# Who issues the row loads of the first expert layer's early tiles, behind which fence, and when the ends of the lists are written

## The chip, the core and the metric

The kernel runs on one core of a Trainium2 chip. The metric is device time in microseconds (us), from one execution of the whole program; lower is better. Before the change three runs took 1994.12, 1999.18 and 2002.74 us; their median, 1999.18 us, is the time before.

The engines are called as the profile calls them: PE (matmul; PEld loads its stationary operand), DVE (vector), ACT (scalar: activation functions, copies), POOL (general purpose; it also issues the indirect transfers here), SP (issues transfers and computes nothing). ACT and SP issue plain transfers. ACTq and SPq mark what the engine's sequencer does: waits, register work, transfers that it issues.

## What is computed

Four layers on 8 x 512 tokens of 256 numbers, each with a residual and a layer norm behind it: three gated recurrent layers, a mixture of 8 experts in which each expert chooses its tokens, attention with a relative bias, and a mixture of 16 experts in which each token has four. Only the second layer and what lies just before it matter here:

```python
probs = softmax(xt @ Wg)                       # 4096 tokens, 8 experts
top_idx = top_k(probs.T, T // E)               # each expert picks 512 tokens
tok2exp = argmax(where(selected, probs.T, -inf), axis=0)   # then each token has one expert
for e in range(E):
    gate = where(tok2exp == e, weights, 0.0)
    out = out + gate[:, None] * (gelu(xt @ W1[e]) @ W2[e])
x = layernorm(x + out)
```

## The kernel before

The program is written in Python and fully unrolled; a scheduler orders the instructions of each engine, except where a block takes the order as written.

**Lists.** Once each token has its expert, the tokens are sorted into lists, one for each expert, in device memory (`m0rows`, class `Lists`). A row is 276 float32 numbers: 256 of the token, its gate and its number. POOL writes the rows with 32 indirect transfers of 128 rows (`put`, L722); each token's place has been computed by DVE (L1113 to L1116, `slot`). A list is rarely a multiple of 128 long, so behind each list's last row 128 empty rows are written (`end_list`, L755 to L759): eight plain transfers by SP, whose address is loaded to a register from the table `m0end` (L750). The lists are then worked on in tiles of 128 rows of one expert. DVE builds a table that says for each tile where its rows begin and which expert's weights it needs (`table`, L781 to L814).

**Early tiles.** Once half of the puts (16) have landed, some tiles are known to be full whatever the other half brings: NE0 = 8 of the 39 tiles are taken from these, the early tiles. Their loads wait for a fence, an instruction that waits for these 16 puts (`fence`, L736 to L746). Before the change it is a copy of one column on ACT (L741), and the loads of the eight early tiles (`load`, L886 to L899) are issued by ACT, those of all later tiles by SP. The later tiles wait for a second fence on POOL (L743, `close`), behind all puts and all ends of lists.

**A tile** (`run`): two transposes of its rows on PE (L903, `m0xp`), a copy to SBUF by DVE (L905, `m0xq`), the first product (L916, `m0h`: four banks of PSUM, eight matmuls, which the trace counts as sixteen), four gelus on ACT that free these banks (L924, `m0hT`), the second product (L938, `m0o`), gate and residual on DVE (L1145, `z`), and an indirect transfer on POOL that puts the rows back in token order (L1148, `res`, called the scatter below). There are only four banks for `m0h`, so the first product of a tile needs the gelus of the tile before it.

**What sets the order.** Four weight buffers (`m0ws`, 1034 KB each) are filled by SP (L882, L884), the first four before all else; a buffer is refilled when the tile four before it is done with it, and from the second round on only if the expert changes. There are five row buffers, so tile 5's load waits for the scatter of tile 0 (which reads its row's token number from that buffer), tile 6's for that of tile 1, and so on. Each engine's instructions run in order, so a load that waits holds back everything behind it on the engine that issues it. In the order of the built kernel, ACT's part is: fence, loads of tiles 0 to 4, table of the gelu function, gelus of tiles 0 to 2, load of tile 5, gelus of tile 3, loads of tiles 6 and 7, gelus of tile 4. SP's part is: weights of tiles 0 to 3, the eight ends of lists (called from `besides` at tile 0), weights of tiles 4 to 7, then a load and its weights in turn. PE's part is: transposes of tiles 0 and 1, first products of tiles 0 and 1, transposes of tile 2, second product of tile 0, first product of tile 2, and so on.

A plain transfer tells of its landing by one of eight semaphores taken in turn, and is not issued before that semaphore's earlier transfer has landed. In the kernel before, the second and third end of a list so wait for ACT's loads of tiles 0 and 1.

Of the kernel before, what the change touches and what calls it, by code (L numbers as in the profile page):

```python
# [46 lines left out]
NE0 = (NC // 2 * P - E0 * (P - 1)) // P  # L47
# [632 lines left out]
class Lists:  # L680
# [53 lines left out]
            tc.declare_no_dep(ins, load, reason="of rows written before")  # L734
        self.written.append(ins)

    def fence(self, on_act=False):

        full = self.rp.tile([P, 1], F32, name=f"{self.name}full{len(self.written)}")
        if on_act:  # L740
            ins = self.nc.scalar.copy(full, self.pno).ins  # L741
        else:
            ins = self.nc.gpsimd.memset(full, 0.0).ins  # L743
        for w in self.written:
            self.tc.add_manual_dep(ins, w.name, SYNC, reason="the lists are full")
        return ins  # L746

# [110 lines left out]
    def run(self, ctx, ident, w_pack, bias, done, taken=None, besides=None):  # L858

        tc, nc, E, NT, nm = self.tc, self.nc, self.E, self.NT, self.name
        table, value, weights_of = self.of, self.value, self.weights_of
        wp = ctx.enter_context(tc.tile_pool(name=f"{nm}w", bufs=1))
        hp = self.hp
        psX = ctx.enter_context(tc.tile_pool(name=f"{nm}psX", bufs=2, space=PSUM))
        psH = ctx.enter_context(tc.tile_pool(name=f"{nm}psH", bufs=4, space=PSUM))
        psO = ctx.enter_context(
            tc.tile_pool(name=f"{nm}psO", bufs=1 if bias else 2, space=PSUM)
        )  # L870
        ws = [None] * len(self.held) + [
            wp.tile([P, WPK], F32, name=f"{nm}ws{i}") for i in range(len(self.held), NW)
        ]
        ws[: len(self.held)] = self.held
        xgs, hTs = {}, {}

        def weights(t):
            if t < len(self.held):
                return
            w = weights_of(t, w_pack)  # L880
            if t - table(t)[0] < NW:
                nc.sync.dma_start(ws[t % NW], w)  # L882
            else:
                nc.sync.dma_start(ws[t % NW], w, cond=value(t, 2, 1))  # L884

        def load(t):  # L886
            xgs[t] = hp.tile([P, RW], F32, tag="xg", bufs=NW + 1, name=f"{nm}xg_{t}")

            q = nc.sync if bias or t >= self.early else nc.scalar
            at = value(t, 0, E * LT, q.engine)  # L890
            ins = q.dma_start(xgs[t], self.rows[bass.ds(at, P), :]).ins
            if t < self.early:

                for w in self.written:
                    tc.declare_no_dep(ins, w, reason="other rows, or before grown")
                tc.add_manual_dep(ins, self.grown.name, SYNC, reason="full tiles")
                self.loads.append(ins)

        def turn(t):  # L899
            xg = xgs[t]  # L900
            ps = psX.tile([P, DC, P], F32, tag="x", name=f"{nm}xp_{t}")
            for dc in range(DC):
                nc.tensor.transpose(ps[:, dc, :], xg[:, dc * P : (dc + 1) * P], ident)  # L903
            xq = hp.tile([P, DC, P], F32, tag="xq", name=f"{nm}xq_{t}")
            nc.vector.tensor_copy(xq, ps)  # L905
            xgs[t] = (xg, xq)

        def first(t):
            xg, xq = xgs[t]
            w = ws[t % NW]  # L910
            hT = hp.tile([P, FC, P], F32, tag="hT", name=f"{nm}hT_{t}")
            for fc in range(FC):
                ps = psH.tile([P, P], F32, tag="h", name=f"{nm}h_{t}_{fc}")
                for dc in range(DC):
                    o = dc * F + fc * P
                    nc.tensor.matmul(  # L916
                        ps, w[:, o : o + P], xq[:, dc, :],
                        start=(dc == 0), stop=(dc == DC - 1),
                    )
                o = DC * F + FC * D + fc  # L920
                if bias:
                    ins = nc.scalar.activation(hT[:, fc, :], ps, AF.Gelu, bias=w[:, o : o + 1])  # L922
                else:
                    ins = nc.scalar.activation(hT[:, fc, :], ps, AF.Gelu)  # L924
            hTs[t] = hT
            if taken:
                taken(t, xg, w)
                xgs[t] = None, None
            return ins.ins

        def second(t):
            xg, _ = xgs.pop(t)
            hT = hTs.pop(t)
            w = ws[t % NW]
            ps = psO.tile([P, D], F32, tag="o", name=f"{nm}o_{t}")
            for fc in range(FC):
                o = DC * F + fc * D
                nc.tensor.matmul(  # L938
                    ps, hT[:, fc, :], w[:, o : o + D], start=(fc == 0), stop=(fc == FC - 1)
                )  # L940
            done(t, xg, ps)


        for t in range(0 if bias else NW):
            weights(t)
        for t in range(NW):
            load(t)
            if bias:
                weights(t)
        turn(0)  # L950
        for t in range(NT + 1):
            if t < NT:
                ins = first(t)
            if t + 1 < NT:
                turn(t + 1)
            if t > 0:
                second(t - 1)
                if t + NW - 1 < NT:
                    load(t + NW - 1)
                    weights(t + NW - 1)  # L960
            if besides and t < NT:
                besides(t, ins)
# [112 lines left out]
def expert_choice_layer(tc, pre, x_ext, lg, ident, a):  # L1075

    nc = tc.nc
    x_tok = x_ext[:, :, :D]
    with ExitStack() as ctx:
        L = Lists(tc, ctx, "m0", E0, NT0, a)  # L1080
        rp = L.rp
        res = L.dram.tile([T + P, D], F32, name="res0")
        psX = pre.enter_context(tc.tile_pool(name="m0psG", bufs=2, space=PSUM))
# [26 lines left out]
        with tc.manual_schedule(engines={mybir.EngineType.DVE}):  # L1110
            for i in range(2):
                k = slice(i * NC // 2, (i + 1) * NC // 2)
                nc.vector.tensor_add(pl[:, k], rk[:, k], cnt.rearrange("p e c -> p c e")[:, k])  # L1113
                nc.vector.tensor_mul(pl[:, k], pl[:, k], M[:, k])
                nc.vector.reduce_sum(fs[:, k], pl[:, k], AX.X)
                nc.vector.tensor_copy(slot[:, k], fs[:, k])  # L1116
            n, half = (rp.tile([P, E0], F32, name=k) for k in ("n0", "half0"))
            nc.vector.tensor_sub(half, upto[:, :, NC // 2 - 1], L.off)
            nc.vector.tensor_sub(n, upto[:, :, NC - 1], L.off)
            for c in range(NC // 2):  # L1120
                L.put(slot[:, c : c + 1], x_ext[:, c, :])
            L.early, L.grown = NE0, L.fence(on_act=True)
            for c in range(NC // 2, NC):
                L.put(slot[:, c : c + 1], x_ext[:, c, :])
            L.done = rp.tile([P, E0], F32, name="done0")
            for _, part in L.table(half, 0, 0) + [L.early_tiles()]:
                part()
            for _, part in L.table(n, P - 1, NE0, L.done):
                part()
            L.ends(n)  # L1130
        pre.close()

        def besides(t, ins):
            if t == 0:
                for e in range(E0):
                    L.end_list(e)

            if t == NE0 - NW:
                L.close()
# [26 lines left out]
        for g in range(NC // 4):  # L1166
            ins = nc.sync.dma_start(
                x_tok[:, g * 4 : (g + 1) * 4, :], src[:, g * 4 : (g + 1) * 4, :]
            ).ins
# [4 lines left out]
class TokenChoice:  # L1174
# [233 lines left out]
    def besides(self, t, ins):  # L1408

        L = self.L  # L1410
        self.put_one(ins)
        if self.todo:
            self.some(1.6, True, True)
            if not self.todo:
                n, count = self.count("n8")
                self.rest = [count, (0.3, lambda: L.ends(n))] + L.table(n, P - 1, NE1, L.done)
                self.ended = 0
        elif self.rest:
            self.rest.pop(0)[1]()
        elif self.ended < E1:  # L1420
            for e in range(self.ended, self.ended + 2):
                L.end_list(e)
            self.ended += 2
        elif not self.puts and self.ended == E1:
            assert t < NE1 - NW - 2
            L.close()
            self.ended += 1
            self.bias_weights()
            self.rest = [(0.7, lambda g=g: self.shares(g)) for g in range(2)]
# [357 lines left out]
def block(tc, a, out, stages=4):  # L1787
    nc = tc.nc
    with tc.tile_pool(name="const", bufs=1) as cp, ExitStack() as rctx:
# [23 lines left out]
        if stages > 1:  # L1813
            expert_choice_layer(tc, pre, x_ext, lg, ident, a)
# [84 lines left out]
```

## Time and profile before

| | us |
|---|---|
| median of the runs | 1999.18 |
| the profiled execution's own time | 2001.2 |
| its span, first to last instruction | 1999.4 |
| PE busy | 1737.9 (87%) |
| DVE busy | 1130.2 (57%) |
| ACT busy | 1004.5 (50%) |
| POOL busy | 515.3 (26%) |
| the first expert layer's tiles: first transpose to last product's end | 494.88 to 664.12 |

The views that are used: the page cuts the span into 40 slices of about 50 us and gives each engine's busy share in tenths. The timeline lists instructions in order of time: start, length, engine, line, operation, what it writes and reads, and in brackets how long the engine was idle before it and what ended that. The view of one line gives, for each operation of that line, how often it ran, its shortest, median and longest duration in ns, and when the first and last began. The view of the queues counts transfers' packets in a stretch: q1 carries what SP issues, q10 what ACT issues, q0 POOL's indirect transfers. The table of stretches gives busy times, PE's granted clock and the DMA engines' share in each.

### The profile page before, as it was taken

The page shows a single profiled execution, that of the slowest core. Times are in us where ns is not written, and L with a number is a line of the kernel's source. Part 1 is how long each engine was busy: PE and PEld are TensorE (multiplying, and loading weights), DVE is VectorE, ACT ScalarE, POOL GpSimd, SP SyncE. Part 2 cuts the span into 40 slices and gives each one's busy share as a digit, 9 for nine tenths or more (in the row PEclk, how much of TensorE's full clock was granted, in tenths as well). Part 3 has the DMA queues.
Part 4 walks back from the last instruction along what each step waited for, and adds up shares of the span by engine and source line. Part 5 has one row for each costly group of instructions (what it writes and reads, how often), then busy time and mean ns, then how long its engine had stood idle before and what let it go on. Part 6 is the DMA issues. An engine that isn't in the chain of part 4 may idle for free. (4 is left out here: it accounts for less than half of the span.)

```text
span 1999.4 us, 31165 instructions
## 1 busy us (share of the span) xinstructions
PE 1737.9 (87%) x10396; PEld 1135.0 (57%) x10396; DVE 1130.2 (57%) x2841; ACT 1004.5 (50%) x2167; POOL 515.3 (26%) x438
## 2 busy tenths in 40 slices
PE   7999995531699698898989998987999999999995
PEld 3555553321699585222222222323889999999994
DVE  6999998853122531676777686884434222222226
ACT  4899976500132421357666767655534334334343
POOL 1000000004222221001041323233566644444440
PEclk8999998655899897899999999998999999999997
DMA  9100000004554400000010111122676767566558
GB/s 358 37 0 1 1 0 1 32 7 167 190 179 144 119 1 19 14 17 17 17 58 17 59 34 42 46 74 74 167 211 128 152 154 188 108 146 141 117 103 255
DMA packets 107102, 179.65 MB, mean 90 GB/s; under 512 B 17005, under 2 KB 86847, under 8 KB 100160
## 3 DMA queue, kind: packets, MB, share of 16 engines
q1 hardware_dynamic: 72608, 128.32, 20.6%
q0 software_dynamic: 30176, 45.59, 11.5%
q10 hardware_dynamic: 4160, 3.76, 0.6%
q8 instruction: 84, 1.38, 0.3%
q14 instruction: 74, 0.61, 0.1%
HBM read 244.79 MB, written 62.98 MB: 154 GB/s over the span
## 5 line engine op out<-in xcount | busy, mean ns | idle before, releaser
L1699 DVE TENSOR_REDUCE nmx<-s 128x1 f32<-128x512 f32 x512 | 330.0, 686 | 161.8 <-PE t L1621 102.0
L1706 ACT ACTIVATE pe<-t 128x512 f32<-128x512 f32 x512 | 278.2, 595 | 210.2 <-PE t L1621 201.8
L1609 PE MATMUL s<-kT,qT 32*128 32x512 f32 x1024 | 304.7, 669 | 54.4 <-ACT pe L1706 25.5
L1621 PE MATMUL t<-qA,kT 32*128 32x512 f32 x1024 | 293.3, 649 | 2.5 <-ACT pe L1706 2.0
L1758 POOL DMA_INDIRECT acc<-y,at x143 | 221.4, 1548 | 259.6 <-DVE at L1751 190.6
L1609 PEld LDWEIGHTS s<-kT,qT 32*128 32x128 f32 x1024 | 82.0, 190 | 221.7 <-ACT pe L1706 174.5
L922 ACT ACTIVATE m1hT<-m1h,m1ws 128x128 f32<-128x128 f32 x284 | 104.0, 369 | 155.2 <-PE m1h L916 133.6
L922 ACT ACTIVATE m1hT<-m1h,xT 128x128 f32<-128x128 f32 x288 | 105.9, 369 | 148.5 <-PE m1h L916 133.6
L1757 DVE TENSOR_SCALAR y<-m1o,gt 128x256 f32<-128x256 f32 x143 | 69.1, 483 | 167.9 <-PE m1o L938 161.1
L905 DVE COPY m1xq<-m1xp 128x256 f32<-128x256 f32 x143 | 60.6, 424 | 180.7 <-PE m1xp L903 96.1
L722 POOL DMA_INDIRECT m1rows<-x_ext,slot x128 | 127.2, 994 | 118.4 <-ACT pe L1706 75.8
L916 PE MATMUL m1h<-m1xq,xT 128*128 128x128 f32 x1152 | 143.5, 278 | 4.7 <-issue 3.0
L916 PEld LDWEIGHTS m1h<-m1xq,xT 128*128 128x128 f32 x1152 | 141.3, 194 | 9.4 <-issue 3.8
L916 PEld LDWEIGHTS m1h<-m1xq,m1ws 128*128 128x128 f32 x1136 | 137.4, 192 | 7.5 <-issue 4.1
L916 PE MATMUL m1h<-m1xq,m1ws 128*128 128x128 f32 x1136 | 138.7, 275 | 2.9 <-DVE m1xq L905 2.2
L1645 PE MATMUL po<-pe,V 128*17 128x512 f32 x1024 | 138.0, 611 | 1.2 <-ACT pe L1706 1.2
L938 PE MATMUL m1o<-xT,m1hT 128*128 128x256 f32 x576 | 138.2, 382 | 0.7 <-issue 0.5
L938 PE MATMUL m1o<-m1ws,m1hT 128*128 128x256 f32 x568 | 134.9, 379 | 0.0
L1675 POOL TENSOR_TENSOR AO<-AO,on 128x256 f32<-128x256 f32 x32 | 23.5, 735 | 353.1 <-DVE on L1670 352.9
L938 PEld LDWEIGHTS m1o<-xT,m1hT 128*128 128x128 f32 x576 | 104.2, 192 | 12.2 <-ACT m1hT L922 0.7
L938 PEld LDWEIGHTS m1o<-m1ws,m1hT 128*128 128x128 f32 x568 | 102.2, 190 | 10.8
L714 POOL MEMSET m0none<- 128x276 f32 x1 | 0.3, 328 | 394.4 <-ACT table L673 394.4
(349 smaller groups left out, 3031.9 us busy)
## 6 DMA issues: line engine op xcount, KB each, us to landing
xT<-in_w_pack SPq DMA_DIRECT2D x72, 1034.0 KB
m1ws<-in_w_pack SPq DMA_DIRECT2D x71, 1034.0 KB
m0ws<-in_w_pack SPq DMA_DIRECT2D x39, 1034.0 KB
m1xg<-m1rows SPq DMA_DIRECT2D x143, 138.0 KB
acc<-zero SPq DMA_DIRECT2D x2, 4096.0 KB
f<-acc SPq DMA_DIRECT2D x16, 512.0 KB
m0xg<-m0rows SPq DMA_DIRECT2D x31, 138.0 KB
xT<-in_xT SPq DMA_DIRECT2D x4, 1024.0 KB
```

Source lines behind the costliest of these rows:

```text
L722: ins = self.nc.gpsimd.indirect_dma_start(out=self.rows[:, :], out_offset=bass.IndirectOffsetOnAxis(ap=place, axis=0), in_=row, in_offset= ...
L905: nc.vector.tensor_copy(xq, ps)
L916: nc.tensor.matmul(ps, w[:, o : o + P], xq[:, dc, :], start=(dc == 0), stop=(dc == DC - 1),)
L922: ins = nc.scalar.activation(hT[:, fc, :], ps, AF.Gelu, bias=w[:, o : o + 1])
L938: nc.tensor.matmul(ps, hT[:, fc, :], w[:, o : o + D], start=(fc == 0), stop=(fc == FC - 1))
L1609: mm = nc.tensor.matmul(ps, qTs[u % NR][r, qc * P : (qc + 1) * P], kTs[u % NR][r, :], start=True, stop=True,)
L1621: mm = nc.tensor.matmul(ps, kTs[v % NR][r, kc * P : (kc + 1) * P], qAs[v][r, :], start=True, stop=True,)
L1645: mm = nc.tensor.matmul(po[h4 * HP : h4 * HP + VW, :], V[:, b * NQ + kc, 4 * g + h4, :], pes.pop((u, kc, h4)), start=(kc == 0), stop=(kc = ...
L1699: ins = nc.vector.tensor_reduce(at, ps, AX.X, ALU.max, negate=True)
L1706: ins = nc.scalar.activation(pe, ps, AF.Exp)
L1757: nc.vector.tensor_scalar_mul(y, ps, gt)
L1758: nc.gpsimd.indirect_dma_start(out=R.acc[t % 2][:, :], out_offset=bass.IndirectOffsetOnAxis(ap=at, axis=0), in_=y, in_offset=None, compute ...
```

## The change

Four things. The first fence moves from ACT to DVE (a memset) and stands behind DVE's tables and `L.ends(n)`; it still waits for the first 16 puts only. The early tiles' loads are issued by SP where the tile's number is even and by ACT where it is odd. The eight ends of the lists are written (`besides(-1, None)`) ahead of the first load instead of behind the first tile; on SP they so stand between the first four weights and the loads. The second expert layer has its call with t < 0 return at once.

```diff
-    def fence(self, on_act=False):
+    def fence(self, first=None):
         full = self.rp.tile([P, 1], F32, name=f"{self.name}full{len(self.written)}")
-        if on_act:
-            ins = self.nc.scalar.copy(full, self.pno).ins
+        if first:
+            ins = self.nc.vector.memset(full, 0.0).ins
         else:
             ins = self.nc.gpsimd.memset(full, 0.0).ins
-        for w in self.written:
+        for w in first or self.written:
             self.tc.add_manual_dep(ins, w.name, SYNC, reason="the lists are full")
...
-            q = nc.sync if bias or t >= self.early else nc.scalar
+            q = nc.sync if bias or t >= self.early or t % 2 == 0 else nc.scalar
...
         for t in range(0 if bias else NW):
             weights(t)
+        if besides:
+            besides(-1, None)
         for t in range(NW):
             load(t)
...
-            L.early, L.grown = NE0, L.fence(on_act=True)
+            L.early, first = NE0, list(L.written)
             for c in range(NC // 2, NC):
                 L.put(slot[:, c : c + 1], x_ext[:, c, :])
...
             L.ends(n)
+            L.grown = L.fence(first)
...
         def besides(t, ins):
-            if t == 0:
+            if t < 0:
                 for e in range(E0):
                     L.end_list(e)
```

In the order of the built kernel this gives, on ACT: loads of tiles 1 and 3 (the registers of the first are loaded ahead of the fence), table of the gelu function, gelus of tiles 0 to 2, load of tile 5, gelus of tiles 3 and 4, load of tile 7, gelus of tile 5. On SP: weights of tiles 0 to 3, eight ends of lists, loads of tiles 0, 2 and 4, weights of tiles 4 and 5, load of tile 6, weights of tiles 6 and 7, then as before. The semaphores fall differently: the first four ends of lists wait for none of the transfers of this stretch, the fifth to eighth for the weights of tiles 0 to 3, and the loads of tiles 0 to 4 for the first five ends of lists. On PE the second product of a tile stands behind the next tile's first product for tiles 0 to 13; before, for tiles 0 to 2 only.

More of the change, by code (lines that the diff above doesn't have):

```diff
@@ L1410, in besides @@
         L = self.L
+        if t < 0:
+            return
         self.put_one(ins)
```

## The prediction

> **What bounds the kernel now.** I began with the page's slices, to find the stretch that the diff touches.
>
> ```profile
> PE   7999995531699698898989998987999999999995
> ...
> DMA  9100000004554400000010111122676767566558
> ```
>
> A slice is 50 us. PE is nearly empty in slices 8 to 10 (400 to 550 us), where tokens are given to experts, lists written and the first tiles begun. From slice 11 PE is full. The timeline of PE from 490 us shows when the tiles run:
>
> ```profile
> 494.88 0.66 PE L903 MATMUL m0xp<-ident,m0xg 128*128 128x128 f32 x2 [29.73 <-DMA m0xg<-m0rows]
> 498.59 0.69 PE L903 MATMUL m0xp<-ident,m0xg 128*128 128x128 f32 x2 [3.05 <-issue]
> 499.07 3.62 PE L916 MATMUL m0h<-m0xq,m0ws 128*128 128x128 f32 x16
> 514.54 3.78 PE L916 MATMUL m0h<-m0xq,m0ws 128*128 128x128 f32 x16 [11.85 <-ACT m0hT L924]
> 518.12 0.48 PE L903 MATMUL m0xp<-ident,m0xg 128*128 128x128 f32 x2
> 518.44 1.89 PE L938 MATMUL m0o<-m0ws,m0hT 128*128 128x256 f32 x8
> ```
>
> Tile 0 is transposed at 494.88, tile 1 only at 498.59, and tile 0's first product waits behind it (499.07). Tile 1's product fills the same four banks and waits 11.85 us for ACT's gelus. The timeline of ACT says where ACT was:
>
> ```profile
> 491.05 0.19 ACT L741 COPY m0full<-m0pno 128x1 f32<-128x1 f32 x1 [86.13 <-DMA m0rows<-x_ext,slot]
> 493.96 18.92 ACTq L891 DMA_DIRECT2D m0xg<-m0rows  x5
> 512.92 1.28 ACT L924 ACT_TABLE_LOAD   x1 [21.68 <-DMA m0rows<-m0none]
> 514.21 0.79 ACT L924 ACTIVATE m0hT<-m0h 128x128 f32<-128x128 f32 x4
> ```
>
> It was issuing five loads, one after the other, for 18.92 us. (The releaser named at 512.92 had nothing to do with it; ACT's own sequencer came free.) Why that takes so long is seen in the view of line 891 from 490 to 515 us, against line 882, four like issues by SP from 470 to 480 us:
>
> ```profile
> L891 ACTq FUSED_REGOPS  x5: 43/700/1397, 492.0 to 511.5; - x5
> L891 ACTq DMA_DIRECT2D m0xg<-m0rows x5: 3/690/700, 494.0 to 512.9; - x5
> ```
> ```profile
> L882 SPq FUSED_REGOPS  x4: 37/37/51, 472.1 to 475.0; - x4
> L882 SPq DMA_DIRECT2D m0ws<-in_w_pack x4: 333/345/469, 472.3 to 477.8; - x4
> ```
>
> A register operation takes 700 ns instead of 37. In the same stretch SP writes the ends of lists at the same crawl (481.75 to 514.18, 32.43 us for eight, 4.05 each; part of it waits). It is no fault of the records alone: the view of the queues finds q10's packets, 144 for each load, in 492 to 494.5, 494.5 to 499, 502 to 504, 508 to 511 and 512 to 514 us.
>
> From there on the tiles are bound by PE: 3.73 us each (518.44, 522.17, 525.90 and, from 546.76, without a gap). Last product: 662.23. 38 steps of 3.73 are 141.74, so 2.05 of the 143.79 us are lost, all at tiles 3 to 7. What follows starts from the last scatters (668.20) and attention keeps PE full, so a shift of this stage should reach the end whole.
>
> **The change, part by part.**
>
> *Fence.* It waits for the same 16 puts, which let ACT go at 491.05. DVE is idle from 475.5 to 495.58, and behind the memset stands only the first tile's copy; so the wait holds up nobody. A copy of 0.19 us gives way to a memset (POOL's of 128x1 takes 0.13): nothing. ACT's other waits and first register load, which stood between fence and first load (491.05 to 492.0), now lie ahead: up to 1 us earlier.
>
> *Ends of lists.* Eight on SP ahead of load 0. At SP's pace in 472 to 475 (0.85 to 1.2 us each) they go from 478 to about 487; the last must also wait for the fourth weight tile, and q1 has only 116 packets left in 488 to 490, so the weights are in by 488. Load 0 then stands ready before the fence falls: cost 0, covered by the puts. Lacking that cover, at 4.05 each, they end at 511 (rival 2). Their transfers: 116 packets in 488 to 490 took 16% of 16 engines, 5.1 us, 44 ns a packet; eight lists are 1152 packets, 3.2 us of all engines, about 6 with the puts on half of them. Load 0 queues behind them in q1 and lands between 493 and 495.5. I take 494.9 for its transpose, as now.
>
> *Loads by two engines.* Load 1 goes out at the fence too, so tile 1's transpose follows tile 0's at 495.6 and tile 0's product starts at 496.1 instead of 499.07: -3.0. ACT issues one more load (tile 3) and then loads the table. Bounds: 0.85 us later at SP's pace, 5.6 at the worst spacing of the row (502 to 508); table done at 493.5 or 498.3. Either is before tile 0's product ends, 499.7, and tile 1's product starts there, not at 514.54: -14.8 in all (11.85 of the stall and the 3.0).
>
> *Clock.* In the table of stretches PE's granted clock is 0.50 up to 515 us, 0.67 in 515 to 520, then 1.00: full speed came 3.8 us after PE had begun to work on end. Now it works on from 495, so tile 1's product lies across the step: between 1.95 us (full) and 3.78; I take 2.8: -1.0. Tile 0's second product starts at 499.7 + 2.8 + 0.3 = 502.8 instead of 518.44: **-15.6**.
>
> *What is late next.* POOL's last put ends at 508.6 and tile 0's scatter stands behind it: 508.7, though its rows are ready at 505.2. Now its landing frees ACT 4.8 us after the issue (521.13 to 525.9); so ACT, at load 5, waits until about 513.4, with tile 3's gelus behind it. PE needs them at 512.0: +1.7. Load 6 on SP waits likewise (to 514.5), the weights of tile 6 behind it; a weight tile issued at 520.36 has its landing in the trace's semaphore records at 524.9, 4.5 us, so 519.4, needed at 521.4: 0, by 2 us. For tiles 4 to 14 a second product later in PE's order leaves a buffer's refill 2 steps (7.5 us) where it had 3 (11.2): a load's wait of 1.3 us, 0.8 for issues and 4.5 to land make 6.6. It fits, by 0.9; I add 1.0 (0 to 4). Against that the 2.05 lost now at tiles 3 to 7 go: **+0.65**.
>
> *Sum.* -15.6 + 0.65 = -15.0, and 2001.2 - 15.0 = 1986.2 by the profiled execution, whose time is 2.0 over the median. I forecast **1986**.
>
> **A rule against it.** The Trainium skill ("DMA: Bandwidth & Descriptors", section "Issuing engines are not separate DMA queues") says that issuing from several engines saves no more than the sequencer's time to start each, usually small. By the usual issue in the rows, 0.35 us, three loads fewer on ACT would save 1 us; by the row of this stretch, 18.92 for five, they save over 10. The rule holds for the transfers; here the sequencer's time is the stall. The skill ("Perfetto Trace Analysis", section "Per-engine timelines") also says that an engine issuing such a transfer locks the one block that makes descriptors. That would slow issues, but register work, which is as slow here, needs no descriptors; so it doesn't explain the crawl, and no row shows whether the crawl comes back with two engines issuing.
>
> **Rivals.**
>
> 1. *The crawl belongs to the stretch, not to ACT's five loads.* ACT and SP crawl until 513 whatever they do. For it: both ended at 512.9 together. Against: SP was quick at 472 to 482 with puts under way. Then ACT's gelus go at up to 1.4 us an instruction, tile 1's come some 4 us late, and SP's weights of tile 4 go out at 510 instead of 505: 3 to 5 of the 15 are given back. 1990.
> 2. *Slower: the ends of lists crawl ahead of load 0.* If SP's 4.05 us each is what a list costs beside the puts, load 0 goes out at 511, tile 0's product starts at 516, and the second product at 522.5, 4 us later than now: 2005. It decides from 3.6 us a list on: (507 - 478.5) / 8, as load 0 at 507 gives today's 518.44. Against it: the first two lists' register work was quick, and the long pauses at the second and third were waits for ACT's loads, which the new order hasn't.
> 3. *The gain is eaten behind.* The weights' and scatters' margins of 1 to 2 us fail at tiles 4 to 14, or the later loads' fence (all puts landed, 511) comes to bind. Tile 8's load is due at 522, so the fence doesn't; some 10 us of waits would be needed: 1996.
>
> **How the numbers follow.** What a measurement can tell from no change is 0.5%, 10 us. The forecast's case runs from 1981 (PE at full clock at once, loads landing at 493, 2 us for the profile's offset) to 1989, chance 0.65; rival 1 0.15, half of it beyond 0.5%; rival 3 0.09; rival 2 0.11. The range goes from 1979 to 1994, to leave out rivals 2 and most of 3. Faster 0.65 + 0.08 = 0.73, same 0.07 + 0.09 = 0.16, slower 0.11.
>
> **What would show it.** In the profile after: the memset at 491; the eight ends done by 488 (else rival 2); table load on ACT before 499, gelus at once; no idle PE of 11.85 us behind tile 0's first product; second product of tile 0 at 503; ACT idle some 4 us before tile 3's gelus; last product near 647. Register operations of 700 ns on ACT behind the table load would speak for rival 1; PE waiting for weights at tiles 6 to 12 for rival 3. The prediction is wrong if tile 0's second product comes after 508, or if the stage's gain is there and the end's is not.

## The result and the profile after

The time did not change: median 2002.12 us (1999.10 to 2004.16) beside 2001.01 us (1994.12 to 2005.11) before, nine runs of each, ratio 1.0009 with a 95% interval of 0.9992 to 1.0026. The profiled execution's span is 2002.4 us, before 1999.4.

Executions differ by some us in when they reach this stage, so from here on I count from the start of POOL's first put (467.77 us before, 467.57 after). "Lost behind" is what is missing between the second products of tile 0 and tile 38 from 38 steps of 3.73 us (141.74).

| us after the first put | before | predicted | after |
|---|---|---|---|
| fence falls | 23.28 | 23.3 | 26.38 |
| tile 0's second product starts | 50.67 | 35.0 | 47.71 |
| lost behind | 2.05 | 2.7 | 3.97 |
| last second product starts | 194.46 | 179.5 | 193.42 |

Of 15.6 us at tile 0's second product 3.0 came, and of 15.0 at the last one 1.0. In the page's slices the stage looks as it did; slice 10 (500 to 550 us) of PE went from 6 to 7:

```profile
PE   6999995531799798998999998987999999999995
...
DMA  9100000005544300000010111122676767566558
```

The timeline of PE after the change, from 484 us:

```profile
497.47 1.09 PE L903 MATMUL m0xp<-ident,m0xg 128*128 128x128 f32 x4 [32.52 <-issue]
498.65 4.35 PE L916 MATMUL m0h<-m0xq,m0ws 128*128 128x128 f32 x20
505.99 1.23 PE L916 MATMUL m0h<-m0xq,m0ws 128*128 128x128 f32 x4 [2.99 <-issue]
512.99 2.07 PE L916 MATMUL m0h<-m0xq,m0ws 128*128 128x128 f32 x8 [5.78 <-ACT m0hT L924]
514.86 0.64 PE L903 MATMUL m0xp<-ident,m0xg 128*128 128x128 f32 x2
515.28 2.36 PE L938 MATMUL m0o<-m0ws,m0hT 128*128 128x256 f32 x8
```

Both tiles are transposed together, and tile 0's product (16 of the 20 matmuls) follows at once, as was meant. But tile 1's product goes bank by bank: four matmuls, then a wait, four more at 505.99, a wait, the last eight at 512.99. It needs the banks that ACT's gelus free. The timeline of ACT:

```profile
494.04 1.26 ACTq L891 DMA_DIRECT2D m0xg<-m0rows  x2
495.34 1.28 ACT L924 ACT_TABLE_LOAD   x1 [90.62 <-DMA m0rows<-m0none]
499.91 0.28 ACT L924 ACTIVATE m0hT<-m0h 128x128 f32<-128x128 f32 x1 [3.29 <-issue]
505.65 0.28 ACT L924 ACTIVATE m0hT<-m0h 128x128 f32<-128x128 f32 x1 [5.47 <-remote]
512.66 0.79 ACT L924 ACTIVATE m0hT<-m0h 128x128 f32<-128x128 f32 x4 [6.73 <-remote]
```

ACT's two loads take 1.26 us, where five took 18.92, and the table is there by 496.6. Then the gelus themselves, 0.28 us each, start 5.7 and 7.0 us apart, though tile 0's product was done by about 502 (an estimate: 16 matmuls took 3.62 us before). (The releaser "remote" names nothing that the trace has.) At 512.66 the crawl ends, and four gelus run in 0.79 us. Before the change it ended at 512.87, and POOL's last put was issued by 508.6 (508.4 after): the end of the crawl has not moved. SP was in it too, by the view of line 891 from 490 to 515 us:

```profile
L891 SPq FUSED_REGOPS  x3: 37/690/701, 490.6 to 501.4; - x3
...
L891 SPq DMA_DIRECT2D m0xg<-m0rows x3: 354/696/1397, 494.0 to 503.5; - x3
```

The second difference is ahead of this. The fence falls 3.1 us later by the table (the timeline of DVE, then that of SP):

```profile
493.95 0.06 DVE L741 MEMSET m0full<- 128x1 f32 x1 [18.70 <-issue]
```
```profile
472.09 3.25 SPq L882 DMA_DIRECT2D m0ws<-in_w_pack  x4
476.11 13.44 SPq L759 DMA_DIRECT2D m0rows<-m0none  x8
```

SP has the eight ends out at 489.5, 1.7 us each, 2.5 us behind the estimate and still ahead of the fence. What they cost is on the queues. In 486 to 494 us the view of the queues had this before (packets, MB, share of 16 engines; q0 are the puts, q1 is SP's):

```profile
q0 software_dynamic: 418, 1.21, 41.1%
q1 hardware_dynamic: 212, 0.57, 18.9%
```

and has this after:

```profile
q1 hardware_dynamic: 1223, 1.59, 61.9%
q0 software_dynamic: 395, 1.18, 44.4%
```

The ends' packets filled the DMA engines just when the sixteenth put had to land.

The third difference lies behind. PE now waits for weights, which it had not done before; the worst is at 551.32:

```profile
551.32 2.02 PE L916 MATMUL m0h<-m0xq,m0ws 128*128 128x128 f32 x16 [2.23 <-DMA m0ws<-in_w_pack]
```

The timeline of SP shows why:

```profile
537.78 0.33 SPq L882 DMA_DIRECT2D m0ws<-in_w_pack  x1
544.74 0.33 SPq L891 DMA_DIRECT2D m0xg<-m0rows  x1
545.64 0.33 SPq L882 DMA_DIRECT2D m0ws<-in_w_pack  x1
```

Tile 10's load (544.74) waited some 6 us for the scatter of tile 5, which POOL had issued at 538.17, and tile 10's weights stand behind it: issued 545.64, used 551.32, 5.7 us later. With two more such waits (0.30 at 579.71, 0.83 at 621.82) it is 3.4 us.

### The profile page after: what moved, and what is told of

It reads as the page before. It is cut to its first block, busy times and chain, and to the rows that moved or that the text cites. A ratio compares the mean times of both kernels' runs of the same rounds, so it can differ in the third digit from the quotient of the medians.

```text
span 2002.4 us, 31165 instructions
## 1 busy us (share of the span) xinstructions
PE 1740.8 (87%) x10396; PEld 1136.6 (57%) x10396; DVE 1129.5 (56%) x2842; ACT 1004.3 (50%) x2166; POOL 515.4 (26%) x438
## 5 line engine op out<-in xcount | busy, mean ns | idle before, releaser
L924 ACT ACTIVATE m0hT<-m0h 128x128 f32<-128x128 f32 x156 | 42.4, 279 | 122.4 <-PE m0h L916 90.9
```

## The experiments

**Theories.** (1) The crawl of SP's and ACT's sequencers is made by POOL's unbroken row of 32 puts; who issues the loads only decides whose instructions crawl. (2) It comes from two engines issuing plain transfers at once. (3) It comes from the transfers of the lists' ends. The first four kernels ran against these.

| | fence | tile 0's 2nd product | lost behind | last 2nd product | ratio to before (95%) |
|---|---|---|---|---|---|
| before | 23.28 | 50.67 | 2.05 | 194.46 | 1 |
| after | 26.38 | 47.71 | 3.97 | 193.42 | 1.0009 (0.9992 to 1.0026) |
| after, puts paced | 26.13 | 35.59 | 14.40 | 191.73 | 0.9994 (0.9978 to 1.0011) |
| before, puts paced | 22.91 | 33.01 | 16.84 | 191.59 | 0.9983 (0.9966 to 0.9999) |
| after, ends behind | 22.49 | 47.21 | 2.59 | 191.54 | 0.9994 (0.9980 to 1.0008) |
| after, all loads by SP | 26.00 | 47.80 | 3.17 | 192.71 | 1.0008 (0.9994 to 1.0022) |
| after, gaps between puts | 26.22 | 35.86 | 14.81 | 192.41 | one run, 1996.58 us |
| 24 puts first | 32.08 | 41.85 | 4.04 | 187.63 | 0.9966 (0.9955 to 0.9978) |
| 20 puts first | 27.37 | 36.13 | 6.42 | 184.29 | 0.9944 (0.9923 to 0.9965) |
| the same again | 27.35 | 37.05 | 4.48 | 183.27 | 0.9939 (0.9926 to 0.9952) |
| before, 20 puts first | 27.18 | 37.43 | 5.30 | 184.47 | 0.9954 (0.9939 to 0.9969) |
| 20 first, ends ahead | 28.41 | 38.36 | 6.18 | 186.28 | 0.9965 (0.9951 to 0.9979) |

(The first four columns are us from each kernel's own profiled execution; all but "lost behind" are counted from its first put. One execution stands for each kernel; the two of the kernel with 20 first differ by 0.9 us at tile 0's second product and by 1.0 at the last one.)

**The changed kernel with paced puts.** The last 16 puts come four behind each of tiles 0 to 3's gelus.

```diff
-            for c in range(NC // 2, NC):
-                L.put(slot[:, c : c + 1], x_ext[:, c, :])
...
+            if 0 <= t < 4:
+                for c in range(NC // 2 + 4 * t, NC // 2 + 4 * t + 4):
+                    put = L.put(slot[:, c : c + 1], x_ext[:, c, :])
+                    tc.add_manual_dep(put, ins.name, SYNC, reason="not all rows at once")
```

> The changed kernel, with the last 16 puts not back to back: four behind each of tiles 0 to 3's gelus. Theory 1 (the crawl of SP's and ACT's sequencers is made by POOL's unbroken row of puts): it ends about 4 us after the sixteenth put, so by 494 us; SP's list ends are done before 489, the five loads' issues by 496, ACT's gelus of tiles 0 to 3 follow within 1 us of PE's first products, tile 0's second product starts at 500 to 504 us instead of 515.3, and the time is 8 to 14 us below the kernel before. Theory 2 (two engines issuing at once crawl): register operations of 700 ns stay on both until the last early load is out, about 510 us, second product at 513 to 516, time within 3 us of the changed kernel. Theory 3 (the lists' ends make it): as theory 2 up to 500, then quick.

The crawl went with the puts. POOL issues nothing between 487.6 and 501.65 us, and in that stretch register operations on SP and ACT take 18 to 143 ns from 490 on, some 2 us behind the sixteenth put. PE's timeline:

```profile
497.37 5.47 PE L916 MATMUL m0h<-m0xq,m0ws 128*128 128x128 f32 x32
...
502.90 1.89 PE L938 MATMUL m0o<-m0ws,m0hT 128*128 128x256 f32 x8
```

Both first products run through, and tile 0's second product starts 35.59 us after the first put: what I had predicted for the change itself (35.0). Two engines were issuing, and all eight ends stood ahead, so theories 2 and 3 fall here. But the time stayed where it was: theory 1's 8 to 14 us were missed. Nine transfers of POOL in a row follow from 501.65 to 512.83, and ACT's timeline shows a gap like those of the crawl again (tile 3's product had begun at 509.40, its first gelu comes at 515.40). That this gap is the crawl is argued: ACT's register operations at 509.19 and 510.92 took 37 and 29 ns.

```profile
510.99 0.35 ACTq L891 DMA_DIRECT2D m0xg<-m0rows  x1
515.40 0.28 ACT L924 ACTIVATE m0hT<-m0h 128x128 f32<-128x128 f32 x1 [6.29 <-remote]
```

PE then waits for ACT's gelus (4.79 us up to 518.16), for weights (2.60 at 546.27) and in shorter pieces; in all 14.4 us are lost behind.

**The kernel before with paced puts.** The same edit on the kernel before.

> The kernel before, with the last 16 puts paced the same way. Theory 1: ACT's five loads go out in 2 to 5 us behind its fence instead of 18.9, the table is loaded by 500, tile 1's first product starts at about 503 instead of 514.5 and the second product of tile 0 at 506; 8 to 13 us off the time, within 4 us of the paced changed kernel: then the crawl is what the change meant to go round, and who issues the loads is worth only 3 us. Theory 2 or 3: the five loads still take over 15 us (SP's list ends stand beside them as before); time as before within 4 us.

The mechanism was as theory 1 has it (ACT's five loads in 4.23 us instead of 18.92, tile 0's second product at 33.01, better than expected), the time was not: 16.84 us are lost behind. While POOL issued nine transfers in a row (496.28 to 507.5), ACT's gelus of tile 2 came 1.4 us apart (502.08, 503.52, 504.94, 506.38), and PE stood still for 5.86 us up to 509.01 and 6.36 up to 524.81.

**The changed kernel with the ends behind tile 0.**

```diff
-            if t < 0:
+            if t == 0:
                 for e in range(E0):
                     L.end_list(e)
```

> The changed kernel with the ends of the lists back behind tile 0. If the lists' transfers held up the puts' landing, the fence on DVE falls at 491.0 instead of 493.95 and tile 0's transpose comes 2 to 3 us earlier (494.5 to 495.5 instead of 497.5). Theory 1: the crawl still ends at 512.7, tile 0's second product at 512 to 516, time within 3 us of the changed kernel. Theory 3 (the lists' ends make the crawl): ACT's gelus of tile 0 are quick, second product at 500 to 505, 8 us or more off.

The fence is back at 22.49, so the ends ahead had cost it 3.9 us (3.1 against before). The table says the same throughout: with 16 puts first it falls at 26.00 to 26.38 in the four kernels with the ends ahead, and at 22.49 to 23.28 in the three without. The crawl stayed: ACT's gelus at 492.64, 498.68 and 508.49, tile 0's second product at 47.21. Theory 3 falls again. The earlier fence was worth half a us at that product, since the crawl's end sets it.

**All early loads by SP.** ACT issues no transfer in the stretch.

```diff
-            q = nc.sync if bias or t >= self.early or t % 2 == 0 else nc.scalar
+            q = nc.sync
```

> The changed kernel with all early loads issued by SP, so that ACT issues no transfer in the stretch. Theory 1: ACT's gelus of tiles 0 to 2 crawl all the same, 5 to 7 us apart, until 512.7, and tile 0's second product starts at 513 to 517; time within 3 us of the changed kernel. Theory 2: with one engine issuing, ACT's gelus follow PE's first products within 1 us, second product at 501 to 505, and the time is 8 us or more below the kernel before.

ACT crawls all the same:

```profile
498.17 0.28 ACT L924 ACTIVATE m0hT<-m0h 128x128 f32<-128x128 f32 x1 [32.22 <-PE m0xp L903]
502.09 0.28 ACT L924 ACTIVATE m0hT<-m0h 128x128 f32<-128x128 f32 x1 [3.65 <-PE m0h L916]
509.80 0.79 ACT L924 ACTIVATE m0hT<-m0h 128x128 f32<-128x128 f32 x4 [7.43 <-remote]
```

POOL's last put was issued by 505.4 here, and the crawl ended at 509.8: 4.4 us behind it, as before (512.87 and 508.6) and after (512.66 and 508.4). SP's five loads took 18.21 us. So what ACT issues neither makes the crawl nor lengthens it. Tile 0's second product, at 512.42, and the gaps between the gelus, 3.9 and 7.7 us, lie just outside what theory 1 had (513 to 517, and 5 to 7).

**Gaps between the puts.** Is it the number of puts or their pace? POOL clears a spare tile ahead of each of the last 16 (and POOL's order in this block is taken as written, so that the clearing stands between the puts).

```diff
+            gap = rp.tile([P, 1024], F32, name="gap0")
             for c in range(NC // 2, NC):
+                nc.gpsimd.memset(gap, 0.0)
                 L.put(slot[:, c : c + 1], x_ext[:, c, :])
```

> The changed kernel with POOL clearing a spare 128x1024 tile (0.95 us by its rows of that size) ahead of each of the last 16 puts, so that these come every 2.2 to 2.4 us instead of every 1.28 and end at about 524 us instead of 508. If the crawl needs an unbroken row of puts (1 in 1.28 us): register operations back under 150 ns by 494, ACT's gelus of tile 0 quick, tile 0's second product at 500 to 505 as in the paced kernel. If any put under way makes it: gelus 3 to 7 us apart until 528, second product of tile 0 at 512 to 525. Either way tile 5's load waits for tile 0's scatter, which stands behind the last put, so the stage's end is 0 to 15 us later than in the changed kernel.

The puts came every 2.11 us instead of every 1.28, by POOL's timeline:

```profile
499.80 0.97 POOL L722 DMA_INDIRECT m0rows<-x_ext,slot  x1 [0.17 <-issue]
500.77 0.97 POOL L1127 MEMSET gap<- 128x1024 f32 x1
501.90 0.97 POOL L722 DMA_INDIRECT m0rows<-x_ext,slot  x1 [0.17 <-issue]
```

and the view of line 891 from 490 to 515 us, with puts under way all that time, has register operations as they should be:

```profile
L891 SPq FUSED_REGOPS  x4: 37/37/42, 490.2 to 509.8; - x4
```

Tile 0's second product starts at 35.86. It is the pace. Nor is it the load on the DMA engines. In the table of stretches their busy share (the last number but one) is higher here than in the changed kernel, in the same 5 us. After the change:

```profile
505.00:510.00 5.00, 1.23 (x4) 0.93 (x4) 0.00 (x0) 0.28 (x1) 2.78 (x3) 0.60 0.31 113
```

With gaps:

```profile
505.00:510.00 5.00, 5.00 (x37) 4.73 (x36) 1.39 (x3) 1.11 (x4) 4.67 (x5) 1.00 0.74 241
```

Yet in the changed kernel a register operation at 507.70 takes 700 ns, while with gaps those of SP and ACT take 37 to 133. (In 510 to 515 us the changed kernel's share is 0.00, and the crawl still lasts until 512.66.) Of the 14.81 us lost behind, most are one wait: PE stands still for 12.35 us up to 525.42, since ACT waits at tile 5's load for tile 0's scatter, which stands behind the last put. The stage's end, expected 0 to 15 us later than in the changed kernel, is 1.0 us earlier. I take no verdict on the time from one run.

**24 and 20 puts first.** While no tile runs, the crawl holds up no tile. So these versions put more of them ahead of the fence, which makes more tiles early (16 and 12), and leave few beside the tiles: 8 puts one behind each of tiles 0 to 7, or 12 behind tiles 0 to 8 (two at tiles 0, 3 and 6). Each list's end goes out behind one of tiles 0 to 7. For 20:

```diff
+NK0 = 20
-NE0 = (NC // 2 * P - E0 * (P - 1)) // P
+NE0 = (NK0 * P - E0 * (P - 1)) // P
...
-            nc.vector.tensor_sub(half, upto[:, :, NC // 2 - 1], L.off)
+            nc.vector.tensor_sub(half, upto[:, :, NK0 - 1], L.off)
-            for c in range(NC // 2):
+            for c in range(NK0):
```

> The changed kernel with 24 puts in a row instead of 16 ahead of the fence, so that 16 tiles instead of 8 are early; the other 8 puts one behind each of tiles 0 to 7, and one list's end behind each of these tiles. POOL then has two transfers in 3.73 us while the tiles run, not three. Theory 1 (unbroken puts make the crawl, and it costs wherever they stand beside tiles): the fence falls some 32 us after the first put (22.4 for 16 puts, 8 x 1.28 more), tile 0's second product 9 to 10 us behind it, no crawl from there on, and no stall over 1 us but for weights: the last product starts 184 to 188 us after the first put, against 194.5 before and 193.4 in the changed kernel; 6 to 10 us off the time. Rival (any put beside the tiles brings the crawl): stalls of over 5 us at tiles 1 to 8, last product 193 us or more after the first put, time as before within 4 us.

> As the kernel with 24 puts first, but 20 first (12 early tiles), and the other 12 behind tiles 0 to 8, one or two each: two or three transfers of POOL in 3.73 us. Theory 1: the fence 27.5 us after the first put, tile 0's second product at 37 us after it, last product 179 to 186 us after it: 8 to 14 us off the time. If three transfers in 3.73 us already bring the crawl, stalls of 2 to 6 us at tiles 0, 3 and 6, and the gain is that of the other kernel or less. Rival: as there.

> The kernel with 20 puts first once more, beside the two that differ from it by one part each, for a narrower interval: 0.992 to 0.996 of the kernel before.

Most steps came as theory 1 had it: fence at 32.08 and 27.37, last second product at 187.63 and 184.29, median 1991.94 us beside 1998.71 with 24 first (expected 6 to 10 us less), 1986.46 beside 1998.71 and, again, 1987.16 beside 1998.37 with 20 first (expected 8 to 14). One did not: with 24 first PE waits 2.53 us for a load at 550.28, where no stall over 1 us was expected but for weights. The gains are small, 0.3 to 0.6%, but their intervals are clear of 1, and the changed kernel's is not. The view of the loads' line (892 in this kernel) with 20 first, 490 to 515 us:

```profile
L892 SPq FUSED_REGOPS  x3: 37/37/37, 494.5 to 508.8; - x3
L892 ACTq FUSED_REGOPS  x3: 37/37/37, 494.5 to 514.2; - x3
```

Later single operations of 0.7 to 0.8 us come back on SP (two issues at 528.91 and 529.84, behind a row of three transfers of POOL).

**The kernel before with 20 puts first.** With the crawl out of the way, what is the change worth? Fence and all early loads are back on ACT.

> The kernel before (fence on ACT, all early loads on ACT) with 20 puts first, the other 12 and the lists' ends spread over the early tiles as in the kernel with 20 first. With the crawl gone ACT's five loads take about 4.2 us, as in the paced kernel of before, where tile 0's second product came 10.1 us behind the fence; in the kernel with 20 first it was 8.8. Theory 1: what this case's change is worth by itself, without the crawl, is these 1.3 us and what ACT loses by issuing loads 5 to 11 in line with its gelus, 0 to 4 us: the time lies 1 to 5 us above the kernel with 20 first and 6 to 11 below the kernel before. Rival (issuing on two engines is what brings the gain): time as the kernel before within 4 us.

Tile 0's second product comes 10.25 us behind the fence, with the change 8.76 and 9.70. The median is 1991.94 us beside 1987.16 with the change, but the ratios' intervals (0.9939 to 0.9969, 0.9926 to 0.9952) overlap, and the last second product differs by 0.2 and 1.2 us. So the fence on DVE and the issuing by two engines together bring 0.2 to 1.5 us in the stage, which can hardly be told from the 0.9 and 1.0 by which two executions of one kernel differ; whether they bring more in the time these runs don't settle. The rival is refuted: most of the gain is here without it.

**20 puts first, ends ahead.**

```diff
-            for e in {0: (0,), 1: (1,), 2: (2,), 3: (3,), 4: (4,), 5: (5,), 6: (6,), 7: (7,)}.get(t, ()):
+            for e in {-1: (0, 1, 2, 3, 4, 5, 6, 7)}.get(t, ()):
                 L.end_list(e)
```

> The kernel with 20 puts first, but the ends of the lists ahead of the first load, as the change puts them. In the kernels with 16 first they moved the fence from 22.4 to 26.3 us after the first put. If it is their transfers beside the puts that do this, the fence comes 30 to 31.5 us after the first put instead of 27.4, register operations of 700 ns are seen on SP between the ends, tile 0's second product comes 3 to 4 us later, and the time is 2 to 4 us above the kernel with 20 first. If not, both agree within 1 us.

The fence moved by 1.0 us only, not 3 to 4: the ends are out by 488.6 here, when three of the 20 puts are still to be issued, so their packets, which in the view of 486 to 494 us are still q1's bulk (1203), have mostly passed when the twentieth lands, at 495.6 by the fence. (That this is why the delay is smaller is argued, not tested.) Register operations of 700 ns are seen between the ends, as expected (483.53, 485.66). The last second product comes 2.0 to 3.0 us later and the median is 5 us higher (1992.21 beside 1987.16). The direction was right, the delay of the fence a third of what was expected; the two ratios' intervals just touch.

## Why the prediction was wrong

The step that failed is "gelus at once", and behind it the cost in *Loads by two engines*: I took ACT's crawl for something that its five loads brought with them and that went with them. I wrote that the table would be loaded by 498.3 and that tile 1's product "starts there, not at 514.54"; the table was loaded at 496.6, and the gelus came 5.7 and 7.0 us apart. Rival 1 (the crawl belongs to the stretch) was the case, and I gave it 15 chances in 100. I had set against it that SP was quick at 472 to 482 with puts under way. That was thin: between its quick operations at 482 and the slow ones at 495.6, SP stood in a wait, and the trace says nothing of its pace there. And the crawl doesn't begin with the row of puts: in nine of the twelve kernels the first operation of some 0.7 us on SP comes 5.7 to 9.2 us after the first put (476.76 in the changed kernel), so quick ones at 472 to 475 say nothing against it. Rival 2 was not the case: a list's end took 1.7 us, and 3.6 were needed.

- *Fence, "nothing".* Wrong by 3.1 us. Putting it on DVE cost nothing; what held it was the next point.
- *Ends of lists, "cost 0, covered by the puts".* SP's time was covered (out at 489.5, estimate 487). But I let only load 0 queue behind these transfers, and not the puts for which the fence waits. With the ends behind, the fence falls at 22.49.
- *Loads by two engines, -14.8.* The loads and the joint transposes came as described, and with the puts paced or with gaps tile 0's second product starts at 35.59 and 35.86 against 35.0 predicted. So the mechanism was right for a kernel without the crawl; in this one 3.0 us were left of it. That the number fits so well is in part luck: with the puts paced tile 0's first product starts at 30.06 where I had 28.3, as the fence falls late, and from there to its second product it takes 5.5 us where I had 6.7.
- *Clock, -1.0.* Right in kind where PE works on, and too small: in the table of stretches the paced kernel's granted clock is 0.92 in 500 to 505 us and 1.00 in 505 to 515, and its two first products take 5.47 us, so that of tile 1 some 1.9 (an estimate, with 3.62 for that of tile 0 as before) where I had 2.8. In the changed kernel PE waits, and it falls back from 0.74 (500 to 505) to 0.60 and 0.50.
- *Late next, +0.65.* Too small: 3.97 us are lost behind instead of 2.05, +1.9. The term for weights (1.0) measured 3.4; a weight transfer took 5.7 us to be of use where I had 4.5, behind a load that had waited 6 us for a scatter.
- *Rival 1's price* (1990) was wrong as well: I let each gelu crawl by up to 1.4 us; it was 5.7 and 7.0, and the stage kept 1.0 of 15.0 us.
- *From the stage to the end.* From the last second product's start to the span's end it is 1337.2 us before and 1341.4 after, and the other profiled executions lie between 1332.7 and 1341.0. A us at the stage's end can't be seen in the time of one execution. The 10 us that 20 puts first bring at the stage's end are there: 11 to 12 in the median. My sum also starts from the profiled execution's time (2001.2); from the median it gives 1984, not 1986.

On the rule that I weighed: the Trainium skill ("DMA: Bandwidth & Descriptors", section "Issuing engines are not separate DMA queues") has it that issuing from several engines saves just the sequencer's time, usually little. I let the slow row overrule it. The kernels with 20 puts first agree with the rule: from the fence to tile 0's second product, 0.6 to 1.5 us is all that two engines bring (the fence's place included), once the issues take their usual time.

What stays open: by what path POOL's puts slow the two sequencers (no run tells), why the crawl sets in some us into the row, why in some executions they are slow from 470 or 476 us on and in others quick until 482 with the same puts, and whether the recording has a part in it, since every execution here has its span and clock recorded. That puts every 1.28 us bring it and that 2.11 us are harmless is shown; the limit between them is not.

## What to carry to other kernels

When several sequencers are slow at the same time and recover together, look for what runs through the whole slow stretch on a third engine, and end or thin that out in an experiment, before moving work from one slow queue to another. Put bursts of indirect transfers where no tile needs small instructions on other engines, and thin them beside tiles. A wait that moves by many us at the head of a pipeline is worth only what the queues behind it (a fence, a scatter that frees a buffer, the next weights) let through.

## What the hardware showed

- In a row of POOL's indirect transfers of 128 rows, one every 1.28 us, many operations of SP's and ACT's sequencers took 0.7 or 1.4 us (a register operation else 0.04), from 5.7 to 9.2 us into the row in nine of the twelve kernels (in the kernel before not yet at 15), until some 2 us after a row of 16 and 4.3 to 4.7 us after a row of 32; issued every 2.11 us, the same transfers had no such effect. After a wait the first few go quickly again: in the changed kernel ACT's register operations at 494.81 and 494.88 took 37 and 29 ns, SP's at 495.12 took 690. POOL kept its 1.28 us meanwhile, and DVE's two copies of a tile took 0.85 us as in the paced kernel.
- An engine that issues no transfer is slowed as well: ACT's gelus of 0.28 us started 3.9 and 7.7 us apart with all loads on SP.
- Eight plain transfers of 128 rows of 1104 bytes, 1024 packets, held up a fence that waits for indirect transfers under way beside them, on another queue, by 3.1 to 3.9 us; where three more puts were issued behind them it was 1.0.
